# Two graph attention layers on one core: a prelude with another order of weight loads, strip copies and products

## The chip, the cores and the metric

The kernel runs on one core of a Trainium2 chip. The metric is the device time of one execution in microseconds (us); "before" and "after" are the same computation with and without the change. Lower is better. Single runs of this kernel differ by some per cent, so medians of several runs are compared.

## The reference

```python
def gnn0(x, adj):                       # Wf, Wg, W: 1024 x 1024
    f, g = x @ Wf + bf, x @ Wg + bg
    e = relu(f @ g.T)
    a = softmax(where(adj > 0, e, -9e15), axis=1)
    return a @ (x @ W + bW)

def gnn1(x, adj):                       # W1: 1024 x 1024, a1, a2: 1024 x 1
    h = x @ W1
    e = leaky_relu(h @ a1 + (h @ a2).T, 0.2)
    a = softmax(where(adj > 0, e, -9e15), axis=1)
    return relu(a @ h)

x = layernorm(x + gnn0(x, adj))
x = layernorm(x + gnn1(x, adj))
```

x is 2708 x 1024 in float32, adj is 2708 x 2708 in int32, mostly zero: a row has some 10 to 40 neighbours. Everything is float32.

## The kernel before, in words

The kernel does not multiply whole score matrices. It first makes, for every row, a list of its neighbours (at most CAP = 40), ranks the rows by the length of their lists into 85 groups of 32, and then gathers only the listed rows of x. The scores of layer 0 are x M x^T with M = Wf Wg^T, so that one product per row block, Fr, replaces f and g; the dots of Fr with the gathered rows are DVE's, the weighted sums of the gathered rows TensorE's.

All this change lies in the **prelude** (lists, ranks and M) and in the first steps of layer 0 behind it, together the first 250 us of the run. The prelude's work by engine:

- **adj blocks.** adj is cut into 21 full blocks of 128 rows (`full` = 21) and a short one of 20 rows. SP loads a full block (1354 KB) into one of BUFS = 4 buffers (`load_adj`, line 236). `keys` (550) has ACT turn it into float and sum each row, and POOL multiply it by a descending ramp, so that a neighbour becomes a key that tells its column. `maxima` (568) has DVE take the eight largest keys of each of 16 segments of a row (16 MAX8), and `best` (558) the 40 largest of these 128 (5 MAX8, 4 replacements) into L. `mixed` (577) weaves the MAX8 of one block with the `best` of the block before. The short block is laid out as 4 x 32 rows of 677 columns (`load_short` 595, `short_keys` 602, `short_maxima` 608), and its own `best` is woven in two blocks later. `keep_lists` (621) has ACT write a block's list in its final form and send it to memory.
- **M.** Wf and Wg come in 16 strips of 128 rows (512 KB) into KEPT = 5 slots (`load_weights`, 242), in the order Wg 0 to 3, Wf 0 to 5, Wg 4, Wf 6, Wg 5, Wf 7, Wg 6, Wg 7. `turned` (443) transposes a strip: 8 transposes on TensorE into two PSUM tiles called pt, which ACT copies into Wt (from Wf) or into a half of WgT (tiles halfT). `m_product` (466) makes 128 rows of M for one half of the columns in two times four matmuls; `c_product` (477) makes the bias rows, which ACT copies to cb and rb. The generator `weights` (510) is the order of all this: each `yield` tells a nominal length in us, and `work(upto)` (540) writes out steps until their nominal sum `spent` reaches `upto`. The copies that a step needs from ACT are kept in `late` and written out when the next step is. The bounds given to `work` thus set how the steps of M stand among the blocks' work, on each engine.
- **Ranks.** When all lists are made, `ranks` (326) works on DVE with three small products on TensorE; it stops at marks ("sums", "first", "hot", "second", "third", "end"), and `rank_to` (649) runs it to a mark. "first" is the place behind the first small product, "second" behind 22 small matmuls. It ends with ids and idq, the row numbers that the gathers use.
- **u rows.** `checks` (423) and `u_dots` (197) follow on DVE: each row strip of W1 is multiplied by a1 and a2. W1's strips 0 to 4 are loaded into the five strip slots, 5 and 6 into an adj buffer (lines 684 to 696), 7 into Wt when M is done (712).

Each engine runs its instructions in the order in which the program writes them (the class InOrder, line 61, adds that order as a dependency; nearly every instruction is therefore recorded on line 71). An instruction that waits holds everything behind it on its engine. SP's DMAs go round eight lanes, each of which waits for its last transfer.

The main loop (662) takes block b: ACT's and POOL's `keys(b + 2)`, lists of block b − 3, DVE's `mixed(b)`, the load of block b + 4 into the buffer that this frees, and then `work(6.2 * b - 6.0)`. Behind the loop come the ranks, with `work(124.0)` after the sums (697) and `work(135.0)` after the hot lists (703), and the rest of M in `work(1000.0)` (711).

Layer 0 starts with `load_x(1)` (1163), the gather of 128 rows of x by ids on POOL. Its tile xb lies at an address that an adj buffer had in the prelude. `half_product` makes the two column halves of x M for the first block, `take_half` (1184) copies a half into Fr, four copies for each of its four strips of 32 rows. DVE's first dots need Fr.

Of the kernel before, what the change touches and what calls it, by code (L numbers as in the profile page):

```python
# [8 lines left out]
F32 = mybir.dt.float32  # L9
# [97 lines left out]
def listed_path(ctx, tc, x, adj, Wf, bf, Wg, bg, W, bW, W1, a1, a2, out):  # L107

    nc = tc.nc
    P = 128  # L110
    N, D = x.shape
    KC = D // P
# [20 lines left out]
    pe, dve, act, pool, sp = (InOrder(tc, e) for e in (nc.tensor, nc.vector, nc.scalar, nc.gpsimd, nc.sync))  # L133
# [56 lines left out]
    M = wm.tile([P, KC, D], F32, name="M")  # L190
# [4 lines left out]
    Wt = s0s.enter_context(tc.tile_pool(name="w0", bufs=1, side="right")).tile([P, KC, D], F32, name="Wt")  # L195
# [23 lines left out]
    KEPT, BUFS = 5, 4  # L219
    with ExitStack() as prelude:  # L220
# [3 lines left out]
        stage, adjp = new_pool("stage", KEPT), new_pool("adjp", BUFS)  # L224
# [17 lines left out]
        def load_weights(upto):  # L242
            while len(loaded) < min(upto, len(order)):
                w, k = order[len(loaded)]
                t = stage.tile([P, D], F32, name="rows")
                sp.dma_start(t, w[k * P:(k + 1) * P, :])
                loaded.append(t)
# [190 lines left out]

        at = iter(range(len(order)))

        late, holders, WgT = [], [], {}

        def turned(dst):

            if any(take in holders for take in late):
                for take in late:
                    take()
                late.clear()
            n = next(at)
            t, pts = loaded[n], []  # L450
            for k0 in range(0, KC, 4):
                pt = ps_t.tile([P, 4, P], F32, name="pt")
                for i in range(4):
                    pe.transpose(pt[:, i, :], t[:, (k0 + i) * P:(k0 + i + 1) * P], ident)
                pts.append(pt)
            load_weights(n + 1 + KEPT)

            def take():
                for k0, pt in zip(range(0, KC, 4), pts):
                    act.copy(dst[:, k0:k0 + 4, :], pt)  # L460
            late.append(take)
            holders.append(take)
# [3 lines left out]
        def m_product(k, h):  # L466

            pm = ps_m.tile([P, H, 512], F32, name="pm")
            for i in range(KC):
                if i == KC // 2:  # L470
                    yield 3.5
                pe.matmul(pm[:, 0, :], Wt[:, i, k * P:(k + 1) * P], WgT[h][:, i, :],
                          start=(i == 0), stop=(i == KC - 1))
            late.append(lambda: act.copy(M[:, k, h * 512:(h + 1) * 512], pm[:, 0, :]))
            yield 3.5

        def c_product():

            pm = ps_m.tile([P, H, 512], F32, name="pm")
            for i in range(KC):  # L480
                if i == KC // 2:
                    yield 3.5
                for v, h in ((0, 0), (0, 1), (1, 0), (1, 1)):
                    j = 32 * (2 * v + h)
                    pe.matmul(pm[j:j + 32, 0, :], (bfc, bgc)[v][:, i:i + 1].to_broadcast([P, 32]),
                              Wt[:, i, h * 512:(h + 1) * 512] if v else WgT[h][:, i, :],
                              start=(i == 0), stop=(i == KC - 1))

            def take():
                for h in range(H):  # L490
                    act.copy(cb[32 * h:32 * h + 1], pm[32 * h:32 * h + 1, 0, :])
                for q in range(Q):
                    for h in range(H):
                        act.copy(rb[32 * q:32 * q + 32, h * 512:(h + 1) * 512], pm[64 + 32 * h:96 + 32 * h, 0, :])
            late.append(take)
            yield 3.5
# [13 lines left out]
        def weights():  # L510

            WgT[0] = wt0.tile([P, KC, 512], F32, name="halfT0")
            for k in range(4):
                turned(WgT[0][:, :, k * P:(k + 1) * P])
                yield 1.2
            WgT[1] = wt1.tile([P, KC, 512], F32, name="halfT1")
            turned(Wt[:, :, :P])
            yield 1.2
            for k in range(KC):
                if k + 1 < KC:  # L520
                    turned(Wt[:, :, (k + 1) * P:(k + 2) * P])
                    yield 1.2
                product = m_product(k, 0)
                yield next(product)
                if k >= 4:
                    turned(WgT[1][:, :, (k - 4) * P:(k - 3) * P])
                    yield 1.2
                yield next(product)
                if k == 0:
                    pt = ps_t.tile([P, 4, P], F32, name="pt")  # L530
                    pe.transpose(pt[:, 0, :16], two, ident[:16, :16])
                    late.append(lambda: act.copy(cols.rearrange("p v k -> p (v k)"), pt[:, 0, :16]))
                    holders.append(late[-1])
            yield from c_product()
            for k in range(KC):
                yield from m_product(k, 1)

        work_steps, spent = weights(), [0.0]

        def work(upto):  # L540

            while spent[0] < upto:
                old = list(late)
                spent[0] += next(work_steps, 1000.0)
                for take in old:
                    if take in late:
                        late.remove(take)
                        take()
# [46 lines left out]
        def load_short():  # L595

            for q in range(Q):
                sp.dma_start(short.bitcast(I32)[32 * q:32 * q + 32, :], adj[N - 32:N, q * PART:(q + 1) * PART])
            for h in range(H):
                sp.dma_start(cb[64 + 32 * h:65 + 32 * h], bW.rearrange("(o d) -> o d", o=1)[:, h * 512:(h + 1) * 512])  # L600
# [57 lines left out]
        keys(1)  # L658
        fill_highs()
        work(6.0)  # L660
        load_short()
        for b in range(full - 1):
            if b + 2 < full:
                keys(b + 2)
            if b == 3:
                short_keys()
            if b > 2:
                keep_lists(b - 3)
            if b == 9:
                keep_lists(NB - 1)  # L670
            others = [rest]
            if b == 4:
                short_maxima()
            if b == 6:
                others += [best(NB - 1, last, cand_s), short_total()]
            rest = mixed(b, *others)
            if b == 9:
                for t, a in ((u1b, a1), (u2b, a2)):
                    sp.dma_start(t, bass.AP(tensor=a.tensor, offset=a.offset, ap=[[0, P], [1, D]]))
            if b + BUFS < full:  # L680
                at_once(load_adj(b + BUFS))
            work(6.2 * b - 6.0)
            if b == full - 4:
                w1_rows = [stage.tile([P, D], F32, name="rows") for k in range(KEPT)]
                for k, t in enumerate(w1_rows):
                    sp.dma_start(t, W1[k * P:(k + 1) * P, :])

        t = adjp.tile([P, N], F32, name="adj")
        for k in range(KEPT, KC - 1):
            w1_rows.append(t[:, (k - KEPT) * D:(k - KEPT + 1) * D])  # L690
# [3 lines left out]
        keep_lists(full - 3)  # L694
        b = full - 1
        rank_to("sums")
        work(124.0)
        rank_to("first")
        at_once(rest)
        keep_lists(b - 1)  # L700
        final = maxima(b)
        rank_to("hot")
        work(135.0)
        rank_to("second", iter([next(final) for i in range(6)]))
        rank_to("third")
        rank_to("end", final)
# [43 lines left out]
    def half_product(pm, h, n, xT, w, row=None):  # L750
        c = slice(h * 512, (h + 1) * 512)
        for k in range(KC):
            pe.matmul(pm[:n, h, :], xT[:, k, :n], w[:, k, c],
                      start=(row is None and k == 0), stop=(k == KC - 1))
# [313 lines left out]
    with s0s:  # L1068
# [104 lines left out]
        halves = [ps_m.tile([P, H, 512], F32, name="pm") for h in range(H)]  # L1173
        xT1 = xTs.pop(1)
# [9 lines left out]
        def take_half(copy, ks, h):  # L1184
            c = slice(h * 512, (h + 1) * 512)
            for k in ks:
                for p in range(Q):
                    copy(Fr[1, k][32 * p:32 * p + 32, c], halves[h][32 * k:32 * k + 32, h, :])

        take_half(act.copy, (0, 1), 0)  # L1190
        take_half(act.copy, (2, 3), 0)
        xTs[2] = tp.tile([P, KC, P], F32, name="xT")
        turn2 = turn(xb[2], nrows[2], xTs[2])
        next(turn2)
        half_product(halves[1], 1, P, xT1, M, 0)
        q_dot(1)
        parts = xp.tile([P, D], F32, name="xb")
        small_f = split_product(xTs.pop(0), M, parts, 0, ps_s.tile([P, H, 512], F32, name="po"))
# [1 line left out]
        take_half(act.copy, (0, 1), 1)  # L1200
        for _ in turn2:
            pass
        next(small_f)
        take_half(act.copy, (2, 3), 1)
        f_product(2)
# [36 lines left out]
        for k, u in enumerate(units):  # L1242
            nxt = units[k + 1] if k + 1 < len(units) else None
            b = u.b
# [71 lines left out]
        b = NB - 1  # L1316
# [10 lines left out]
    with ExitStack() as s1s:  # L1327
# [106 lines left out]
        for n, (u, ks) in enumerate(parts):  # L1434
            b, po = u.b, banks[:, n % 2, :]
# [20 lines left out]
            if ks[-1] + 1 == u.G:  # L1456
                k = done1[b]
# [387 lines left out]
```

## Time and profile before

| what | us |
|---|---|
| median of three runs | 1885.37 |
| the three runs | 1868.06, 1885.37, 1900.10 |
| the profiled execution's own time | 1889.49 |
| its span, first to last instruction | 1887.8 |
| block 4's MAX8 start on DVE | 52.38 |
| TensorE: bias rows (c_product) | 115.82 to 122.8 |
| ranks start on DVE | 149.37 |
| gather of the first rows of x on POOL | 194.63 |
| first dots on DVE | 223.09 |

The profile is of one execution, and its own time is 1.7 us over its span. An engine's row in the timeline gives start, length, engine, line, operation, output and input, and in brackets how long the engine stood idle before it and what released it. In the waits, `A <- B: 25.2, 4, 19.1` means that A waited for B four times, 25.2 us in all and 19.1 at most. In the names, xb are the gathered rows of x, pt and pm PSUM tiles, adj a block of adj, cand the 128 candidates of a row, u2b the tile in which the short block lies until a2 is loaded there.

### The profile page before, as it was taken

The numbers are of one execution on the slowest core, as the hardware profiler recorded it, in microseconds if no ns is written. First come the engines' busy times: TensorE is split into PE (matmuls) and PEld (weight loads), VectorE is DVE, ScalarE is ACT, GpSimd is POOL, SyncE is SP. The second block draws the span as 40 slices with busy tenths as digits, with TensorE's granted clock in tenths as the row PEclk, the third lists the DMA queues.
The fourth block names the chain that finished last, engine by engine and source line by source line (L and its number), as shares of the span: only waits on it lengthen the run. The fifth ranks groups of instructions, "written<-read, shape, count | busy, mean of one in ns | idle before, by whom it ended". The sixth has DMA issues, their size and how long they took to land. (4 is left out here: it accounts for less than half of the span.)

```text
span 1887.8 us, 22782 instructions
## 1 busy us (share of the span) xinstructions
PE 1614.6 (86%) x6873; PEld 684.2 (36%) x6873; DVE 1279.9 (68%) x4158; ACT 637.6 (34%) x886; POOL 1180.3 (63%) x1130
## 2 busy tenths in 40 slices
PE   3898759788999999999999998279898988989896
PEld 2443324333443444444444443023333333323332
DVE  5996648767888888888888767246445445545543
ACT  5571425434554544444555551011111111111111
POOL 8892673555676777766767631666666666666630
PEclk7999889888999999999999999589999999989998
DMA  9671583656787778887777863999989999999950
GB/s 365 227 284 50 193 293 116 223 176 238 284 278 270 277 251 274 280 281 262 262 257 263 310 239 136 342 329 320 321 319 348 351 347 317 343 333 352 341 190 35
DMA packets 150961, 503.95 MB, mean 267 GB/s; under 512 B 32714, under 2 KB 32730, under 8 KB 148398
## 3 DMA queue, kind: packets, MB, share of 16 engines
q0 software_dynamic: 131648, 428.27, 63.9%
q1 hardware_dynamic: 16128, 73.71, 10.5%
q8 instruction: 56, 0.92, 0.2%
q10 hardware_dynamic: 3054, 0.43, 0.1%
q14 instruction: 75, 0.61, 0.1%
HBM read 510.81 MB, written 33.75 MB: 288 GB/s over the span
## 5 line engine op out<-in xcount | busy, mean ns | idle before, releaser
L71 POOL DMA_INDIRECT ring<-in_x_dram,SL x405 | 447.2, 1104 | 210.7 <-issue 95.1
L71 DVE SCALAR_TENSOR_TENSOR j<-ring,Fr 128x1024 bf16<-128x1024 f32 x402 | 493.1, 1227 | 100.3 <-ACT Fr L71 41.9
L71 PE MATMUL po<-ring,st 128*32 128x512 f32 x2616 | 376.9, 629 | 109.9 <-issue 56.2
L71 ACT COPY Fr<-pm 32x1024 f32<-32x1024 f32 (+2 forms) x353 | 340.6, 965 | 15.1 <-remote 6.5
L71 POOL DMA_INDIRECT ring<-T,SL x249 | 246.9, 992 | 122.9 <-issue 64.5
L71 PE MATMUL pm<-M,yT 128*128 128x512 f32 (+1 forms) x704 | 318.2, 601 | 4.5 <-issue 3.0
L71 PE MATMUL pm<-Wt,xT 128*128 128x512 f32 (+1 forms) x704 | 305.8, 603 | 12.2 <-issue 12.2
L71 PE MATMUL pm<-M,xT 128*128 128x512 f32 x672 | 298.5, 603 | 2.4 <-issue 2.4
L71 PEld LDWEIGHTS po<-ring,st 128*32 128x32 f32 x2616 | 109.4, 115 | 322.3 <-issue 258.6
L71 POOL DMA_INDIRECT more<-T,SL x156 | 155.0, 993 | 76.9 <-issue 42.8
L71 PEld LDWEIGHTS pm<-M,yT 128*128 128x128 f32 (+1 forms) x704 | 127.7, 187 | 195.7 <-issue 192.9
L71 PEld LDWEIGHTS pm<-Wt,xT 128*128 128x128 f32 (+1 forms) x704 | 131.2, 189 | 175.0 <-issue 171.1
L71 ACT ACTIVATE scores<-scores 128x12 f32<-128x12 f32 (+9 forms) x65 | 14.0, 216 | 520.2 <-DVE scores L71 415.2
L71 PEld LDWEIGHTS pm<-M,xT 128*128 128x128 f32 x672 | 130.5, 194 | 160.9 <-issue 158.2
L71 POOL TENSOR_TENSOR adj<-adj,iota 128x2708 f32<-128x2708 f32 (+2 forms) x23 | 124.5, 5446 | 17.0 <-ACT adj L71 17.0
L71 ACT ACTIVATE y<-po,ri 128x512 f32<-128x512 f32 (+1 forms) x88 | 58.1, 684 | 211.7 <-remote 134.4
L71 PE MATMUL pm<-halfT,Wt 128*128 128x512 f32 x256 | 114.3, 602 | 0.0
L71 POOL DMA_INDIRECT SL<-LD,idq x85 | 88.4, 1040 | 28.4 <-issue 25.8
L71 PE MATMUL po<-more,st 128*32 128x512 f32 x624 | 94.0, 659 | 13.2 <-issue 13.1
L71 DVE MAX8 cand<-adj 128x8 f32<-128x170 f32 x336 | 95.9, 325 | 12.4 <-POOL adj L71 12.4
L71 ACT COPY xT<-pt 128x512 f32<-128x512 f32 (+2 forms) x109 | 47.9, 499 | 85.6 <-PE pt L71 56.7
L71 POOL DMA_INDIRECT z<-in_x_dram,ids x21 | 25.1, 1194 | 81.3 <-DVE j L71 26.3
(236 smaller groups left out, 1436.0 us busy)
## 6 DMA issues: line engine op xcount, KB each, us to landing
adj<-in_adj_dram SPq DMA_DIRECT2D x19, 1354.0 KB
X1S<-z SPq DMA_DIRECT2D x19, 512.0 KB
ring<-in_x_dram,SL POOLq DMA_INDIRECT x405
rows<-in_L_gnn_Wg_dram SPq DMA_DIRECT2D x8, 512.0 KB
rows<-in_L_gnn_Wf_dram SPq DMA_DIRECT2D x8, 512.0 KB
M<-in_L_gnn_W_dram SPq DMA_DIRECT2D x1, 4096.0 KB
ring<-T,SL POOLq DMA_INDIRECT x249
u1b<-X1S SPq DMA_DIRECT2D x7, 512.0 KB
```

The costliest lines, as they stand in the source:

```text
L71: made = self.tc.keep_in_program_order(op(*args, **kwargs))
```

## The change

The strips of weights are no longer asked for by the transposing of an earlier strip but one or two a block, right behind the load of an adj block, and never more than five ahead of those transposed. The copies of Wf's strip 0 are written out before the loop. The short block is loaded at block 1, its MAX8 stand at block 6 and its `best` at block 8, each two later, as are the last block's `keep_lists` and the loads of a1 and a2. Wf's strip 1 is transposed behind the first half of M's first product. The bounds of `work` in the loop are 16 us higher, up to 118.0; `work(124.0)` is gone, and 135.0 becomes 128.0. One more adj tile is named before the one that takes W1's strips. In layer 0 the second column half of the product is written before the transposes of the third block's rows, and the copies of Fr's strip 3 after them.

```diff
--- before.py
+++ after.py
@@ -438,7 +438,7 @@
 
         at = iter(range(len(order)))
 
-        late, holders, WgT = [], [], {}
+        late, holders, WgT, turned_so_far = [], [], {}, [0]
 
         def turned(dst):
 
@@ -447,13 +447,14 @@
                     take()
                 late.clear()
             n = next(at)
+            load_weights(n + 1)
             t, pts = loaded[n], []
             for k0 in range(0, KC, 4):
                 pt = ps_t.tile([P, 4, P], F32, name="pt")
                 for i in range(4):
                     pe.transpose(pt[:, i, :], t[:, (k0 + i) * P:(k0 + i + 1) * P], ident)
                 pts.append(pt)
-            load_weights(n + 1 + KEPT)
+            turned_so_far[0] = n + 1
 
             def take():
                 for k0, pt in zip(range(0, KC, 4), pts):
@@ -517,11 +518,14 @@
             turned(Wt[:, :, :P])
             yield 1.2
             for k in range(KC):
-                if k + 1 < KC:
+                if 0 < k and k + 1 < KC:
                     turned(Wt[:, :, (k + 1) * P:(k + 2) * P])
                     yield 1.2
                 product = m_product(k, 0)
                 yield next(product)
+                if k == 0:
+                    turned(Wt[:, :, P:2 * P])
+                    yield 1.2
                 if k >= 4:
                     turned(WgT[1][:, :, (k - 4) * P:(k - 3) * P])
                     yield 1.2
@@ -658,7 +662,9 @@
         keys(1)
         fill_highs()
         work(6.0)
-        load_short()
+        for take in late:
+            take()
+        late.clear()
         for b in range(full - 1):
             if b + 2 < full:
                 keys(b + 2)
@@ -666,25 +672,29 @@
                 short_keys()
             if b > 2:
                 keep_lists(b - 3)
-            if b == 9:
+            if b == 11:
                 keep_lists(NB - 1)
             others = [rest]
-            if b == 4:
+            if b == 6:
                 short_maxima()
-            if b == 6:
+            if b == 8:
                 others += [best(NB - 1, last, cand_s), short_total()]
             rest = mixed(b, *others)
-            if b == 9:
+            if b == 11:
                 for t, a in ((u1b, a1), (u2b, a2)):
                     sp.dma_start(t, bass.AP(tensor=a.tensor, offset=a.offset, ap=[[0, P], [1, D]]))
             if b + BUFS < full:
                 at_once(load_adj(b + BUFS))
-            work(6.2 * b - 6.0)
+            if b == 1:
+                load_short()
+            load_weights(min(KEPT + b + 1 + max(0, b - 3), turned_so_far[0] + KEPT))
+            work(min(6.2 * b + 10.0, 118.0))
             if b == full - 4:
                 w1_rows = [stage.tile([P, D], F32, name="rows") for k in range(KEPT)]
                 for k, t in enumerate(w1_rows):
                     sp.dma_start(t, W1[k * P:(k + 1) * P, :])
 
+        adjp.tile([P, N], F32, name="adj")
         t = adjp.tile([P, N], F32, name="adj")
         for k in range(KEPT, KC - 1):
             w1_rows.append(t[:, (k - KEPT) * D:(k - KEPT + 1) * D])
@@ -694,13 +704,12 @@
         keep_lists(full - 3)
         b = full - 1
         rank_to("sums")
-        work(124.0)
         rank_to("first")
         at_once(rest)
         keep_lists(b - 1)
         final = maxima(b)
         rank_to("hot")
-        work(135.0)
+        work(128.0)
         rank_to("second", iter([next(final) for i in range(6)]))
         rank_to("third")
         rank_to("end", final)
@@ -1188,11 +1197,11 @@
                     copy(Fr[1, k][32 * p:32 * p + 32, c], halves[h][32 * k:32 * k + 32, h, :])
 
         take_half(act.copy, (0, 1), 0)
-        take_half(act.copy, (2, 3), 0)
+        take_half(act.copy, (2,), 0)
+        half_product(halves[1], 1, P, xT1, M, 0)
         xTs[2] = tp.tile([P, KC, P], F32, name="xT")
         turn2 = turn(xb[2], nrows[2], xTs[2])
         next(turn2)
-        half_product(halves[1], 1, P, xT1, M, 0)
         q_dot(1)
         parts = xp.tile([P, D], F32, name="xb")
         small_f = split_product(xTs.pop(0), M, parts, 0, ps_s.tile([P, H, 512], F32, name="po"))
@@ -1200,6 +1209,7 @@
         take_half(act.copy, (0, 1), 1)
         for _ in turn2:
             pass
+        take_half(act.copy, (3,), 0)
         next(small_f)
         take_half(act.copy, (2, 3), 1)
         f_product(2)
```

## The prediction

> **What bounds the kernel now.** The page comes first: its engine line and the chain that ended last.
>
> ```profile
> PE 1614.6 (86%) x6873; PEld 684.2 (36%) x6873; DVE 1279.9 (68%) x4158; ACT 637.6 (34%) x886; POOL 1180.3 (63%) x1130
> PE 33%; issue 5%; DVE 2%; DMA 1%; ACT 1%; POOL 1%; another core or an unknown queue 0%; POOLq 0%; DVEq 0%; ACTq 0%
> ```
>
> TensorE sets the long stretch: it is busy 86% and leads the chain. The change touches only the first 262 us of 1887.8. There TensorE is busy 9.6 of the first 40 us and 30.3 of the 50 us from 150 to 200 (the windows view), so other waits set the pace. I ask the waits of that stretch next (what waits, for whom: us in total, times, longest).
>
> ```profile
> POOL xb L71 <- DVE iota L71: 40.6, 1, 40.6
> PE pt L71 <- ACT Wt L71: 25.2, 4, 19.1
> POOL adj L71 <- ACT adj L71: 17.0, 9, 4.3
> DVE j L71 <- ACT Fr L71: 14.5, 1, 14.5
> DVE halfT L71 <- PE pt L71: 14.1, 2, 8.0
> DVE u2b L71 <- POOL u2b L71: 11.0, 1, 11.0
> ```
>
> Read backwards, they name the path: the first dots on DVE wait for Fr (14.5), Fr for the gather of x, the gather for DVE (40.6), and DVE, while ranking, twice for TensorE (14.1). Before that DVE waits for POOL's short block (11.0). TensorE waits 19.1 for one copy by ACT. The timeline by engine shows why (start, length, what, idle before it and its releaser).
>
> ```profile
> 38.44 1.97 PE L71 MATMUL pt<-ident,rows 128*128 128x128 f32 x8 [19.13 <-ACT Wt L71]
> 57.02 1.04 PE L71 MATMUL pt<-ident,rows 128*128 128x128 f32 x8
> 164.18 13.98 PE L71 MATMUL pm<-halfT,Wt 128*128 128x512 f32 x32
> ```
>
> ```profile
> 35.36 2.46 ACT L71 ACTIVATE adj<-adj 128x2708 f32<-128x2708 int32 x1 [9.27 <-DVE cand L71]
> 37.82 1.05 ACT L71 COPY Wt<-pt 128x512 f32<-128x512 f32 x2
> ```
>
> ```profile
> 28.70 6.22 SPq L71 DMA_DIRECT2D adj<-in_adj_dram  x3
> ```
>
> The copy of Wf's strip 0 (37.82) stands behind ACT's work on block 4 of adj (35.36). That block's load goes out only at 28.70, behind five strips of Wf and the short block's loads on SP's queue. TensorE loses 19 us and then trails with M to the end of the ranking, where two of its products stand in front of the ranks' own small ones:
>
> ```profile
> 51.41 1.05 DVE L71 MAX8 u2b<-u2b 128x8 f32<-128x170 f32 x4 [10.97 <-POOL u2b L71]
> 164.40 0.39 DVE L71 TENSOR_TENSOR halfT<-halfT,pt 128x220 f32<-128x220 f32 x1 [6.09 <-PE pt L71]
> 179.32 0.24 DVE L71 COPY halfT<-pt 64x85 f32<-64x85 f32 x1 [8.02 <-PE pt L71]
> ```
>
> ```profile
> 101.86 29.65 POOL L71 TENSOR_TENSOR adj<-adj,iota 128x2708 f32<-128x2708 f32 x5 [2.63 <-ACT adj L71]
> 194.63 2.08 POOL L71 DMA_INDIRECT xb<-in_x_dram,ids  x1 [40.57 <-DVE iota L71]
> ```
>
> A block costs POOL 29.65/5 = 5.93 us and DVE about as much: from 52.38 DVE has work without a break to the ranks at 149.37, 97.0 us with the short block's own list.
>
> **The sum** is made on the profiled execution: 1889.5 us, span 1887.8 and 1.7 around it, 4.1 above the median of three, 1885.4.
>
> **Loads, Wf0's copies, second strip.** The same strips and blocks are loaded, in another order. Block 4 needs only the buffer of block 0, whose last MAX8 ends at 14.5. An adj block keeps the DMA engines busy some 3.3 us when loads follow one another (successive blocks' landings 20.27 and 23.53), a strip 512/1354 of that, 1.3. So block 3 lands at 23.5, block 4 at 26.9, Wf1 at 28.2, block 5 at 31.6, the four short loads at 32.9, Wf2 at about 34.4. On TensorE five strips are through by 20, the first half of M's step 0 runs 20.4 to 24.0, Wf1 28.2 to 30.1, the second half to 34.0, Wf2 34.4 to 36.2 (1.94 a strip after a wait). ACT has Wf2's two copies before block 4: 36.9. Block 4 then runs on ACT to 39.5 and on POOL to 45.4. That is 39.5 for POOL's start against 37.99: **1.5 later**, the price of the strip in front of it.
>
> **The short block's lists two blocks later.** DVE no longer waits for POOL's product of the short block before block 4. It starts block 4 at 45.4, not 52.38: **−7.0**. Its four MAX8 (1.05) are done at block 6, when their data lies long ready: +1.0 before the ranks. The longer list (best of the short block) and the loads of a1 and a2 move within DVE's unbroken stretch and SP's queue: nothing; there they have until the first u_dots, 187.1 and more. The last block's keep_lists moves too, one ACTIVATE (0.37) and its DMA, in ACT's slack; if ACT had none, 0.4.
>
> **Strips behind adj's loads.** Each later strip is asked for when DVE releases a block, behind that block's load: 5.4 to 6.0 us from issue to ACT's use (58.82 to 64.80, 64.23 to 70.21), then 1.3. By that rule Wf5 lands at 58.3 and is needed at 59.0, Wf6 64.3 (67.6), Wf7 73.7 (76.3), the strips of Wg 3.7 to 9 us ahead. Nothing, but Wf5's cover is 0.7 us; if it is gone every later product is late by as much. TensorE runs from 36.2 through seven products (6.86 each, 48.0), nine strips (0.87 when no wait, 7.8) and the row sums (7.0), to about 99: 23 earlier than 122.8.
>
> **ACT's cluster.** After the row sums ACT copies cb and rb, 1.16 + 4.71 = 5.9 us in one piece. They now come at 100, behind block 14, and block 15's keys end at about 109. POOL, at 5.93 a block from 39.5 and 1.6 for the short one, wants them at 106.1: 2.9 late. DVE runs about 2 behind POOL once it has done the short list, so I take **+1.3** for DVE, between 0 (enough lag) and 2.9 (none). Ranks start at 45.4 + 1.0 + 97.0 + 1.3 = **144.7**, not 149.37.
>
> **M's end in the ranks.** The bounds of TensorE's work change to 118 in the loop, none at "sums" and 128 before "second". Built in this order, 44 matmuls of half 1 stand before the ranks' first product, 12 between it and the second, 8 after. One takes 41.47/48 = 0.86. The 44 are 38 us: over at 138, ten before the sums (144.7 + 3.85 = 148.5), so the first wait (6.09) goes; late next is DVE itself. The 12 are 10.3, from 148.5 to 158.8, and 1.7 for a cold start (16 rows of product took 8.72 after the long wait, 7.03 warm): 160.6. DVE, with neither wait, arrives at 144.7 + 8.94 + 6.9 = 160.5. With the 22 small matmuls (1.19) the copy starts at 161.8, not 179.32: **−17.5**, which holds all terms so far. The other 8 matmuls (6.9, cold 8.6) follow the constant's product at about 166.5 and end at 175; TensorE's next need is x's transposes, 200.25 − 17.5 = 182.8. That cover is 8 us; without it they would cost 6.9. W1's last strip, loaded after them, is needed only after the first dots.
>
> **The new adj tile** before W1's rows. In both built programs the tile that holds W1's rows 5 and 6 covers the same addresses, and the first block's x still overlaps it: the gather still waits for four u_dots (1.27 each). I cost it at nothing; bounds: 0 and, if the gather were free, −6.5 (rival B).
>
> **Order of Fr's copies.** The second half of the product stands behind z's transposes, and one of four groups of copies (4 × 0.59) moves behind x's next transposes. Fr's first strip is whole 2.4 us earlier at most. ACT feeds the dots' 14.5 us wait directly (copies 211.26 to 225.38), so I take **−2.0**, between 0 and −2.4. The fourth group now stands between the second half's; the dots that want it are later than those of strips 0 and 1.
>
> Sum: −17.5 − 2.0 = −19.5; 1889.5 − 19.5 = 1870.0, and 4.1 lower beside the median: **1866**. After the prelude every step follows from the gather of x, so the gain should stay.
>
> Beside the strip's 0.87 and 1.04 us stands a rule that speaks against them. The Trainium skill, "TensorE: Matmul & The Clock Gate", section "Part 4: PE-mode transpose", says that transposes don't count as TensorE work for the fast clock and that the full clock does not engage in them. The trace shows 1.04 right behind products and 1.94 to 1.97 behind waits, so here it disagrees; by the rule the sum would be 1874, as in rival F.
>
> **Rivals.**
> A, the forecast: 1866.
> B, the gather of x is really clear of W1's rows. Then x comes after the ids (165) and M's last copy (175) ends last instead of 182.8: at most 7.8, I take 6.5 more: 1859. For it: the wait of 40.6 is named after DVE's u_dots. Against it: the addresses.
> C, ACT's order paces the blocks. Copies of strips stand ahead of blocks on ACT, so POOL's waits (17.0 in nine pieces) don't shrink but grow. If the ranks start at 152 (7 late, half a us for each block), the rank waits still go: 152 + 3.85 + 12 + 1.2 = 169 against 179.3, −10.3, and Fr −1.5: 1889.5 − 11.8 − 4.1 = 1874.
> D, the other side: a closed loop. DVE frees a buffer, SP loads a block and a strip (5.9 + 1.3), TensorE turns it behind one or two products (2.0 + 6.9 or 13.7), ACT copies (1.1) and only then does the next block's keys (2.65), POOL 5.93: 25.5 or 32.3, against 4 × 5.93 = 23.7 for four buffers. With two products on the way in each turn it is 8.1 a block, 2.15 more; over 13 blocks +28, less the 18 that the rest still brings: 1885.4 + 10 = 1895. It decides from 1.5 us a block. Against it: strips come ahead of need by the working above, so the copies don't wait a whole turn.
> E, the gain is not handed on: the long stretch, led by TensorE, has 28% gaps for other waits that a different start may open: 1885.
> F, strips always at 1.94: nine times 1.07 is 9.6 more before cb and rb, which then meet block 16 or 17, and POOL's wait grows from 2.9 to about 9: some 7.5 of the 19.5 are lost, −12: 1874.
>
> **How the numbers follow.** A 0.55, C 0.20, E 0.08, B 0.07, D 0.06, F 0.04. The likeliest gives 1866. Single runs of before lie from 1868.1 to 1900.1, some 16 us to either side, so a median of a few can miss a true 1866 by about ten. 1848 to 1887 takes in A, B, C, E and F with most of that spread; D and the outer tails are left out, below 2 in 10. Two per cent, about what a measurement of this kernel can tell from no change, is 37.7 us: 1847.7 and 1923.1. Below the first only A's and B's tails lie, 0.11; above the second part of D and a stray median, 0.06; within 0.83.
>
> **What would show it.** Right: TensorE's 19.1 us wait for Wt gone, its transposes of Wf1 near 28; DVE's 10.97 gone and block 4 at about 45; row sums over near 100; POOL waiting for ACT once after cb and rb, about 3; ranks from 144.7 and no wait over 2 us in them for TensorE; x's gather at about 177, still released by DVE; the dots' wait for Fr near 12.5. Wrong: strips that TensorE waits for (C, D), ranks from 149 or later, the gather before the u_dots (B), transposes of 1.9 right behind products (F), or all this and the same total (E).

## The result, and the profile after

| | before | after |
|---|---|---|
| median of 22 runs of each, us | 1889.7 | 1873.3 |
| ratio, with its 95% interval | | 0.9923 [0.9902, 0.9945] |
| span of the profiled execution | 1887.8 | 1869.0 |
| block 4's MAX8 start on DVE | 52.57 | 44.99 |
| bias rows done on TensorE | 122.9 | 100.0 |
| ranks start on DVE | 149.37 | 143.92 |
| copy behind the second mark | 179.32 | 160.88 |
| first gather of x | 194.63 | 176.20 |
| first dots on DVE | 223.09 | 201.86 |
| DVE takes the next rows of x | 262.15 | 242.53 |

The kernel is 0.8% faster, 14.6 us of 1889.7 (10.4 to 18.5 by the interval); the forecast was 19.5 less than before, which from the median of three runs then known (1885.4) gave 1866. The 52.38 of the table before is a MAX8 of block 3's `best`, which stands in front of block 4's first at 52.57. Ratios leave disturbed executions out; the traces of two experiments below, e1_take_back and e7_rank_bounds_only, come from disturbed ones, so only their first 250 us are read.

The waits of the same stretch of the changed kernel, 0 to 262 us (us in total, times, longest):

```profile
POOL xb L71 <- DVE iota L71: 27.7, 1, 27.7
...
POOL adj L71 <- ACT adj L71: 11.7, 4, 4.4
DVE j L71 <- ACT Fr L71: 11.5, 1, 11.5
...
DVE j L71 <- DMA xb<-in_x_dram,ids: 11.1, 1, 11.1
...
PE pt L71 <- DMA rows<-in_L_gnn_Wf_dram: 4.7, 1, 4.7
...
DVE halfT L71 <- PE pt L71: 1.3, 1, 1.3
```

Gone are TensorE's wait for ACT's copy (25.2 in four) and DVE's for the short block (11.0). The ranks' waits for TensorE shrank from 14.1 to 1.3. New is TensorE's wait of 4.7 for Wf's strip 1. The 11.1 that DVE waits for xb is the wait for the second gather of x, behind the first dots (9.5 before). TensorE's timeline, changed kernel:

```profile
28.05 1.94 PE L71 MATMUL pt<-ident,rows 128*128 128x128 f32 x8 [4.67 <-DMA rows<-in_L_gnn_Wf_dram]
...
147.33 0.17 PE L71 MATMUL pt<-halfT,lower 128*128 128x10 bf16 x1 [9.34 <-DVE halfT L71]
...
147.80 11.93 PE L71 MATMUL pm<-halfT,Wt 128*128 128x512 f32 x24
```

TensorE now waits 9.3 us for the ranks; before, the ranks waited for it. (The trace has two records for each of M's matmuls, so x24 are 12 of them.) ACT's, DVE's and POOL's timelines, changed kernel:

```profile
35.40 1.07 ACT L71 COPY Wt<-pt 128x512 f32<-128x512 f32 x2 [0.65 <-PE pt L71]
36.36 2.47 ACT L71 ACTIVATE adj<-adj 128x2708 f32<-128x2708 int32 x1
```

```profile
44.99 0.34 DVE L71 MAX8 cand<-adj 128x8 f32<-128x170 f32 x1 [4.29 <-POOL adj L71]
...
56.51 1.04 DVE L71 MAX8 u2b<-u2b 128x8 f32<-128x170 f32 x4
...
114.65 0.34 DVE L71 MAX8 cand<-adj 128x8 f32<-128x170 f32 x1 [0.90 <-POOL adj L71]
...
160.88 0.24 DVE L71 COPY halfT<-pt 64x85 f32<-64x85 f32 x1 [1.33 <-PE pt L71]
```

```profile
52.37 53.22 POOL L71 TENSOR_TENSOR adj<-adj,iota 128x2708 f32<-128x2708 f32 x9
108.67 35.38 POOL L71 TENSOR_TENSOR adj<-adj,iota 128x2708 f32<-128x2708 f32 x6 [3.09 <-ACT adj L71]
...
176.20 2.09 POOL L71 DMA_INDIRECT xb<-in_x_dram,ids  x1 [27.70 <-DVE iota L71]
```

The short block's MAX8 (56.51) have no wait. POOL runs nine blocks without a break and then waits 3.09 behind ACT's cb and rb; DVE waits 0.90 for the block that this delays (114.65). The gather of x is still released by DVE's product on W1's rows (iota is that product's scrap output).

### The profile page after: what moved, and what is told of

Same layout as the page of the kernel before. It is cut to its first block, busy times and chain, and to the rows that moved or that the text cites. A ratio compares the mean times of both kernels' runs of the same rounds, so it can differ in the third digit from the quotient of the medians.

```text
span 1869.0 us, 22758 instructions
## 1 busy us (share of the span) xinstructions
PE 1609.9 (86%) x6851; PEld 684.0 (37%) x6873; DVE 1277.7 (68%) x4158; ACT 636.5 (34%) x886; POOL 1174.6 (63%) x1130
## 3 DMA queue, kind: packets, MB, share of 16 engines
q1 hardware_dynamic: 16128, 73.71, 10.6%
## 5 line engine op out<-in xcount | busy, mean ns | idle before, releaser
L71 POOL DMA_INDIRECT ring<-in_x_dram,SL x405 | 442.4, 1092 | 213.8 <-issue 94.4
L71 PE MATMUL po<-ring,st 128*32 128x512 f32 x2616 | 366.3, 616 | 103.8 <-issue 42.8
L71 ACT COPY Fr<-pm 32x1024 f32<-32x1024 f32 (+2 forms) x353 | 340.6, 965 | 24.4 <-remote 15.9
L71 PE MATMUL pm<-M,yT 128*128 128x512 f32 (+1 forms) x704 | 324.9, 605 | 16.2 <-issue 14.1
L71 PE MATMUL pm<-Wt,xT 128*128 128x512 f32 (+1 forms) x704 | 299.9, 593 | 3.5 <-issue 2.9
L71 ACT ACTIVATE scores<-scores 128x12 f32<-128x12 f32 (+9 forms) x65 | 14.1, 216 | 549.0 <-DVE scores L71 446.7
L71 PEld LDWEIGHTS pm<-M,xT 128*128 128x128 f32 x672 | 130.4, 194 | 160.9 <-issue 157.9
L71 POOL TENSOR_TENSOR adj<-adj,iota 128x2708 f32<-128x2708 f32 (+2 forms) x23 | 124.3, 5440 | 11.7 <-ACT adj L71 11.7
L71 ACT COPY yT<-pt 128x256 f32<-128x256 f32 (+1 forms) x86 | 27.6, 373 | 136.4 <-PE pt L71 109.7
```

Source lines behind the costliest of these rows:

```text
L71: made = self.tc.keep_in_program_order(op(*args, **kwargs))
```

## The experiments

Three calls of four kernels; those of a call ran on one chip and share its runs of the kernel before. "Gather" is the first gather of x, "dots" the first dots on DVE, in the kernel's trace. Beside them stand the trace of before (194.63, 223.09) and two of the changed kernel (176.20, 201.86; in the third call 178.86, 205.36).

| kernel | ranks | second mark | gather | dots | ratio to before |
|---|---|---|---|---|---|
| e1_take_back | 144.11 | 162.46 | 177.78 | 206.53 | 0.9940 [0.9881, 0.9998] |
| e4_short_only | 141.80 | 171.18 | 186.50 | 216.20 | 0.9990 [0.9937, 1.0043] |
| e5_copies_only | 149.34 | 179.59 | 194.91 | 223.58 | 1.0052 [0.9999, 1.0105] |
| e7_rank_bounds_only | 149.04 | 172.42 | 187.75 | 216.68 | 0.9986 [0.9929, 1.0042] |
| e2_short_back | 154.51 | 171.54 | 186.86 | 212.68 | 0.9978 [0.9944, 1.0013] |
| e9_loads_back | 144.68 | 164.12 | 179.45 | 206.12 | 0.9852 [0.9751, 0.9953] |
| e8_u_first | 144.57 | 163.19 | 173.13 | 196.73 | 0.9891 [0.9850, 0.9932] |
| e10_short_rank | 141.97 | 164.62 | 179.94 | 208.80 | 0.9905 [0.9869, 0.9941] |
| after_again | 144.92 | 163.53 | 178.86 | 205.36 | 0.9902 [0.9885, 0.9919] |
| e11_rank_fill | 144.71 | 160.27 | 175.57 | 202.21 | 0.9900 [0.9886, 0.9914] |
| e12_fill_u_first | 144.18 | 159.74 | 169.66 | 194.75 | 0.9892 [0.9873, 0.9911] |
| e13_delay | 144.28 | 162.75 | 198.34 | 224.91 | 1.0012 [1.0001, 1.0023] |

In the first call the intervals reach some 10 us to either side, so the ratios there can't tell whether a gain of 7 or 8 us at the gather comes out at the end; for single parts only the marks in the traces are read.

### One part alone on the kernel before

**e4_short_only**: the short block's lists two blocks later.

```diff
-            if b == 9:
+            if b == 11:
                 keep_lists(NB - 1)
...
-            if b == 4:
+            if b == 6:
                 short_maxima()
-            if b == 6:
+            if b == 8:
                 others += [best(NB - 1, last, cand_s), short_total()]
...
-            if b == 9:
+            if b == 11:
                 for t, a in ((u1b, a1), (u2b, a2)):
```

> The kernel before with the short block's lists two blocks later and nothing else. Theory that two paths must both be shortened: block 4 starts on DVE at about 45 and the ranks at 143 instead of 149.4, but TensorE is as late as before, so the waits for it grow from 14 to about 20 us and x's gather stays between 191 and 195; total 1886 to 1890. Rival, that DVE's blocks alone set the end: gather at 188.5 and total 1883.

The gather came 8.1 earlier, past both expectations, and the theory is wrong in one half: the ranks start 7.6 earlier, but TensorE's bias rows come 9.5 earlier too (113.4 instead of 122.9), with its order of work untouched. DVE frees the adj buffers sooner, so SP loads and ACT's keys come sooner, and with them the strip copies that stand between the keys. The ranks' waits stay nearly as they were (6.09 and 8.02 before):

```profile
156.26 0.38 DVE L71 TENSOR_TENSOR halfT<-halfT,pt 128x220 f32<-128x220 f32 x1 [5.64 <-PE pt L71]
...
171.18 0.24 DVE L71 COPY halfT<-pt 64x85 f32<-64x85 f32 x1 [8.02 <-PE pt L71]
```

**e5_copies_only**: the copies of Wf's strip 0 before the loop.

```diff
         work(6.0)
+        for take in late:
+            take()
+        late.clear()
         load_short()
```

> The kernel before with the copies of Wf's strip 0 written out before the loop and nothing else. TensorE's wait of 19.1 goes, M's first product comes about 9 earlier, but the next copies still stand behind ACT's block keys. Theory: most of the 9 is lost again by the bias rows (before 115.8 to 122.8), they come 2 to 5 earlier, and x's gather 2 to 5 (190 to 193). Rival, that the one copy is the whole of TensorE's lateness: bias rows 9 or more earlier, gather at 186 or less.

Nothing is left of it; the 2 to 5 us expected were too much as well. TensorE's timeline and its waits for ACT's copies:

```profile
25.07 1.94 PE L71 MATMUL pt<-ident,rows 128*128 128x128 f32 x8 [5.39 <-DMA rows<-in_L_gnn_Wf_dram]
26.81 8.94 PE L71 MATMUL pm<-halfT,Wt 128*128 128x512 f32 x16
```

```profile
PE pt L71 <- ACT Wt L71: 14.9, 5, 8.4
```

The largest wait in TensorE's list was removed and its first product came 13.4 earlier (26.81 for 40.20), yet the bias rows end at 123.2 for 122.9. The next copies stand behind ACT's next keys, and these have not moved: TensorE's other waits for copies grew from 6.1 (25.2 less 19.1) to 14.9.

**e7_rank_bounds_only**: only the bounds behind the loop.

```diff
         rank_to("sums")
-        work(124.0)
         rank_to("first")
...
-        work(135.0)
+        work(128.0)
```

> The kernel before with only the bounds behind the loop changed: no steps of M at the sums, 128 instead of 135 before the second mark. Four steps of 4 matmuls (13.7 us) no longer stand before the ranks' first product, so the first wait (6.1) goes; then five steps (17.2) stand before the second. Theory: second mark at about 170.5 instead of 178.1, x's gather about 7.5 earlier, 187; total about 1880. Rival, that the ranks' order matters only with an earlier TensorE: gather within 2 of 194.6.

Nearly as the theory had it: second mark 172.42 (170.5 expected; 20 matmuls took 17.4), gather 6.9 earlier (7.5 expected).

**e10_short_rank**: the edits of e4_short_only and e7_rank_bounds_only together, and no other.

> The kernel before with the short block's lists two blocks later and the bounds behind the loop changed, nothing else: neither loads nor strip copies nor Fr's order. Measured alone, the two moved x's gather by 8.1 and 6.9. Theory: they add up, since TensorE's 36 matmuls end at 144 ahead of the sums at 145.7, and 20 follow: second mark at 164, gather at 179.5, first dots at 208, total 1871. Rival, that without the earlier copies TensorE stands in the way again: gather 184 or later.

They add up: second mark 164.62, gather 179.94, 14.7 earlier of the full change's 18.4, and the ratio is that of the full change within its interval. The other parts (loads in the loop, strips and copies moved, a higher bound in the loop) brought 1 to 4 us more at the gather (178.86 and 176.20). TensorE's long wait is still there:

```profile
PE pt L71 <- ACT Wt L71: 18.0, 1, 18.0
```

So four fifths of the gain at the gather came without removing it.

### One part taken from the changed kernel

**e2_short_back**: the edits of e4_short_only undone.

> The changed kernel with the short block's lists in the old places (MAX8 at block 4, its best at 6). Theory: block 4 on DVE waits for POOL's short keys again, starts at 53.4 instead of 45.0, one us of MAX8 is then already done, and the ranks start at about 151.3; TensorE is ahead, so x's gather moves as much: 183.5 instead of 176.2, total 1880. Rival, that TensorE's early M alone brings the gain: gather within 2 of 176.

Ranks at 154.51, 3 later than expected and even 5 later than before. POOL's and TensorE's timelines say why:

```profile
72.23 5.95 POOL L71 TENSOR_TENSOR adj<-adj,iota 128x2708 f32<-128x2708 f32 x1 [7.98 <-ACT adj L71]
```

```profile
67.14 1.94 PE L71 MATMUL pt<-ident,rows 128*128 128x128 f32 x8 [8.88 <-DMA rows<-in_L_gnn_Wf_dram]
```

```profile
53.61 6.22 SPq L71 DMA_DIRECT2D u2b<-u2b  x8
59.94 0.41 SPq L71 DMA_DIRECT2D adj<-in_adj_dram  x1
60.45 0.37 SPq L71 DMA_DIRECT2D rows<-in_L_gnn_Wf_dram  x1
```

Rival D's loop is here: DVE waits for the short block, so its eight small copies go out late, at 53.61 on SP's queue, and with them the adj load and Wf's strip behind them. In the kernel before they go out as late (52.49), but there the strips that TensorE turns next (57.02, 64.77) had been asked for long before, and it does not wait for them. Here TensorE waits 8.88 for that strip, ACT's copies wait for TensorE, and POOL's block waits 7.98 for ACT, whose queue has the copies in front. So with the short block in its old place the new rule of loading holds the ranks up. The new rule alone was not run; the time of this kernel (0.9978) can't be told from that of the one before.

**e9_loads_back**: the old rule of loading in the changed kernel.

```diff
             n = next(at)
-            load_weights(n + 1)
...
-            turned_so_far[0] = n + 1
+            load_weights(n + 1 + KEPT)
...
-            load_weights(min(KEPT + b + 1 + max(0, b - 3), turned_so_far[0] + KEPT))
```

> The changed kernel with the old rule of loading (each transposing asks for the strip five ahead, nothing asked for in the loop), everything else as changed. adj block 4 is then behind five strips again and lands at about 35 instead of 27, but Wf's strips are there early, so TensorE does not wait for them. Theory: ACT's block 4 starts at 35 to 37 as it does now (36.4), and all later marks stay within 1.5: gather 175 to 177.5, total 1873. Rival, that the order of loads carries the gain: block 4 late, gather 182 or more.

Ranks at 144.68 and gather at 179.45, between 0.6 and 3.2 later than the two traces of the changed kernel, which differ by 2.7 themselves; at most 177.5 was expected, 182 or more by the rival. Block 4 starts on DVE at 41.9, even 3.1 earlier, and that is lost again at ACT's copies of cb and rb: behind them DVE waits 3.85 (at 115.39), where it waits 0.90 in the changed kernel. The order of the loads carries little or nothing of the gain at the gather; the ratio's interval is too wide to add to that.

**e1_take_back**: Fr's copies and the second column half in the old order.

```diff
-        take_half(act.copy, (2,), 0)
-        half_product(halves[1], 1, P, xT1, M, 0)
+        take_half(act.copy, (2, 3), 0)
...
         next(turn2)
+        half_product(halves[1], 1, P, xT1, M, 0)
...
-        take_half(act.copy, (3,), 0)
```

> The changed kernel with Fr's copies and the second column half in the order of before (part 8 undone). If that order is worth what the two traces show (first dots 21.23 earlier, gather of x 18.43), x's gather stays at 176 and the first dots come 2.8 us later, 204.7 instead of 201.9; the total about 1876. If the 2.8 come from TensorE's clock or the gathers instead, the dots stay at 202 and the total at 1873.

From gather to dots it takes 28.75 (before: 28.46), against 25.66 in the changed kernel's first trace and 26.50 in its second: the new order is worth 2 to 3 us there. From the gather to DVE's use of the next rows of x it is 67.6 (before 67.5) against 66.3 and 65.2, so 1.3 to 2.4 would be left of it 40 us later. But e9_loads_back, which has the new order, takes 68.7 there, so this remainder is not shown. What it is worth at the end, the ratio's interval does not tell.

### Beyond the change

**e8_u_first**: the four products that the gather waits for, ahead of the last block's list.

```diff
         score_constant()
+        junk = iota.bitcast(BF16)[:, :D]
+        u_dots(2 * KEPT, U1, lambda k: w1_rows[k], junk)
         at_once(rest)
         keep_lists(b)
...
-        junk = iota.bitcast(BF16)[:, :D]
         checks()
-        u_dots(2 * KEPT, U1, lambda k: w1_rows[k], junk)
```

> The changed kernel with the four products on W1's strips 5 and 6, for whose tile the first gather of x waits, ahead of the last block's list and the checks (5.5 us of DVE's work). Theory: the gather comes 5.5 earlier, 170.7; x's transposes at 176.3, just behind M's last product (175.7); first dots at 196.4 instead of 201.9; total 1868. Rival, that the lists' gathers or M's last product take its place: dots no earlier than 200.

The gather stands 9.9 behind the second mark, not 15.3, and the dots come at 196.73 as expected. But DVE's timeline goes on with

```profile
245.03 1.23 DVE L71 SCALAR_TENSOR_TENSOR j<-xb,rb 128x1024 bf16<-128x1024 f32 x1 [14.77 <-DMA xb<-in_x_dram,ids]
```

where the changed kernel waits 11.08 until 242.53. The last list goes to memory later (ACT issues it at 176.33 instead of 169.12). The gathers of lists, which read it, gain less than the gather of x: the first comes at 180.54 instead of 182.16, though the gather of x is 3.1 earlier. POOL waits 3.58 before it, and the profile names no releaser, so the late list is the likely cause and not a shown one. POOL's next gather of x is 2.5 later (239.12 for 236.60). The dots were 5 us earlier, the next rows of x were not.

**after_again**, the changed kernel once more, and three variants beside it.

> The changed kernel as it is, beside the three that follow: x's gather at 176 to 178, first dots at 202 to 204, total some 15 below the kernel before.

Gather and dots came 0.9 and 1.4 later than the latest expected, the total 17.0 below the kernel before.

**e11_rank_fill**: TensorE's pause before the ranks filled.

```diff
         rank_to("sums")
+        work(127.0)
         rank_to("first")
...
-        work(128.0)
+        work(134.0)
```

> The changed kernel with 52 of M's matmuls before the ranks' first product (44 now), 8 before the second (12 now), 4 at the end. TensorE stands idle 9.3 us before the sums now and its 12 matmuls then take 11.9 to 13.6 instead of 10.3. Theory: the 8 more end at 145, still ahead of the sums (147.3); the pause shrinks to 2.4 and the 8 go at the warm rate, 6.9; the second mark is DVE's, at 159.6, and x's gather comes at 174.9, 1.3 earlier than in the first trace of the changed kernel and 2.5 to 3 earlier than in those with a slow start. Rival, that the 52 end after the sums: gather at 177 or later.

Gather 3.3 earlier than in after_again, though the 8 matmuls took 8.8 and not 6.9; the ratio is the same, with an interval of 0.0014 (2.4 us) to either side. In its trace all of POOL's gathers are earlier than in after_again's, by 3 to 7 us up to 800 us of the run and by 1.5 to 2.7 behind 950.

**e12_fill_u_first**: both edits.

> Both: 52, 8 and 4 matmuls, and the four products on W1's strips 5 and 6 ahead of the last list. Theory: gather at 169.5 (174.9 less 5.4), M done at about 169, x's transposes at 175, first dots at 193.3; total 5 to 8 below the changed kernel of the same call. Rival, that the gathers of the lists then set the dots: dots at 196 or later.

Gather 9.2 and dots 10.6 earlier than in after_again; the total, expected 5 to 8 lower, the same (0.9892 and 0.9902, 1.7 us apart, each known to 3). Of the 10.6, 3.9 are left where DVE takes the next rows of x (240.10 for 244.04), as in e8_u_first. POOL's gathers of lists and rows are 2.6 to 6.3 earlier until 330 us, and by 433 us 0.3; on the way DVE waits 6.2 us in ten pieces for gathered rows, 1.8 in two in after_again. No version of these beats the changed kernel by more than its interval.

**e13_delay**: 16 more products in front of the gather.

```diff
         checks()
-        u_dots(2 * KEPT, U1, lambda k: w1_rows[k], junk)
+        for i in range(5):
+            u_dots(2 * KEPT, U1, lambda k: w1_rows[k], junk)
```

> The changed kernel with 16 more products on W1's strips 5 and 6 on DVE (the same four, four times again) in front of the first gather of x: a delay of 16 x 1.27 = 20.3 us at the gather and nothing else. It measures what of a shift of the start comes out at the end. Theory of the prediction: all, total 20 above the changed kernel of the same call. Rival, that later stages absorb a part: 10 to 16.

The gather moved by 19.5 from after_again and the time by 19.1 (ratios 1.0012 and 0.9902 of 1734.7) or 20.9 (medians 1737.2 and 1716.3): all of it. So a delay of all gathers on POOL by 20 us comes out in full. That an advance of some us does is not shown by these variants: e11_rank_fill and e12_fill_u_first had the gathers earlier and no lower time that their intervals can tell.

## Why the prediction was right, point by point

- **Path and mechanism.** Right at the ranks and the gather, but TensorE's long wait, which the prediction puts at the start of the path, is not what held the end: e10_short_rank keeps 18.0 of it, e5_copies_only removes it for nothing. What counts is how much of M stands in front of the ranks' products and when DVE is through with the blocks. The ranks and the gather moved as forecast: ranks 143.92 (144.7), second mark 160.88 (161.8), gather −18.4 (−17.5). The gather is still released by DVE's products, so rival B is out; strips never ran at 1.9 right behind products (1.04 a strip), so F is out. E, no gain at all, is out by the interval. Its 28% of gaps is not what the windows give: TensorE is busy 1124.7 of the 1280 us from 600 to 1880, 88%. Of C and D, C's growing waits did not come (POOL's 17.0 in nine became 11.7 in four), and D's loop shows in e2_short_back, where the short block's move is missing (its terms as listed add to 25.8 and 32.6, not 25.5 and 32.3; nothing hangs on that).
- **Loads.** Wf's strip 1 came at 28.05 as worked out, and block 4 on DVE at 44.99 (45.4). e9_loads_back shows that the old rule would have done as well: the prediction did not say so.
- **The short block, −7.0 +1.0.** Right at its place. It is worth more than the prediction's step said: by itself 8.1 at the gather, since TensorE follows DVE through the adj buffers and ACT's queue (e4_short_only).
- **ACT's cluster, +1.3.** POOL waited 3.09 as worked out (2.9), and DVE 0.90 for the block behind it (114.65); in after_again it is 1.5. Right for this kernel, inside the range of 0 to 2.9. The cost hangs on where the blocks stand when the cluster comes: 0.19 in e10_short_rank, 3.9 in e9_loads_back. DVE's only other wait from block 5 to the ranks was 0.62, at 58.36.
- **M's end in the ranks.** The first wait went, the second shrank to 1.33, TensorE waits 9.34. The cold start was put at 1.7; the 12 matmuls took 11.93 to 13.60 in seven traces with the same 44 and 12, against 10.3: 1.6 to 3.3. The 161.8 lies inside what was measured (160.9 to 164.1 where the ranks start at 144 to 145), but that the first trace came within 0.9 of it is in part luck: it has the shortest of these cold starts.
- **Fr's order, −2.0.** The dots gained 2.8 (21.23 − 18.43), outside the 0 to 2.4 given: 16 copies stand before the first dots, not 20, and the first half of the product ran 0.4 faster. But summing this step to the end was not justified: e12_fill_u_first had the dots 10.6 earlier and no lower time that its interval can tell.
- **"The gain should stay."** For the gather's part most of it did, and a delay there comes out in full (e13_delay). Against the 18.4 that the gather gained, the two sets of timed runs give 14.6 (10.4 to 18.5) and, in the third call, 17.0 (14.1 to 19.9; 0.0098 of 1734.7).

The forecast time missed by 7.3 us. Of that 4.3 is the base: the median of before is 1889.7 in 22 runs, not the 1885.4 of three. The rest fits the dots' part (2.0) and the width of the interval, but is not told apart. Single traces have a noise of that size too: between 300 and 430 us the shift of POOL's gathers goes from −20.6 to −8.0 and back to −18 in the first pair of traces, around a copy for which ACT waits 15.9 us (before 6.5) on something that the profile does not name. What that is stays open.

## What to carry to other kernels

The longest wait of an engine need not be worth anything: 19 us of TensorE's were removed alone and nothing came of it, because its next input stood behind work of another engine that had not moved. In a ring of engines that share a few buffers, look for the one whose late release holds the others (here DVE waiting for a small side block), and move that first: with the two bounds behind the loop it gave four fifths of what the whole change gave at the gather. And an earlier first use of a result counts for little if the transfers behind it are not earlier too.

## What the runs showed of the hardware

**The clock after a pause.** Windows of the changed kernel around the sums, and of e11_rank_fill (after the busy times: granted TensorE clock, DMA share, GB/s):

```profile
140.00:145.00 5.00, 0.00 (x0) 0.00 (x0) 4.83 (x23) 0.36 (x1) 4.92 (x3) 0.54 0.18 55
...
148.20:150.00 1.80, 1.80 (x3) 0.75 (x3) 1.63 (x8) 0.00 (x0) 0.30 (x1) 0.50 0.04 6
150.00:152.00 2.00, 2.00 (x5) 0.78 (x4) 1.90 (x6) 0.37 (x1) 0.00 (x0) 0.85 0.02 2
152.00:154.00 2.00, 2.00 (x7) 0.81 (x6) 1.83 (x8) 0.00 (x0) 0.00 (x0) 1.00 0.07 11
```

```profile
145.00:148.20 3.20, 0.69 (x3) 0.17 (x2) 3.12 (x6) 0.00 (x0) 2.98 (x4) 1.00 0.01 1
148.20:150.00 1.80, 1.52 (x4) 0.86 (x4) 1.66 (x8) 0.00 (x0) 1.04 (x2) 0.60 0.03 2
150.00:152.00 2.00, 2.00 (x3) 0.67 (x2) 1.86 (x8) 0.37 (x1) 0.00 (x0) 0.50 0.03 6
152.00:154.00 2.00, 2.00 (x6) 0.95 (x5) 1.90 (x5) 0.00 (x0) 0.00 (x0) 1.00 0.10 16
```

In the long pause the clock is halved, 2.4 us after TensorE's last matmul there, and it is full again 2.8 us after M's work has begun. In e11_rank_fill TensorE stood still only some 3 us (145.6 to 148.6, with two tiny products in between), and the clock was halved all the same, just as the work began again. So filling the pause to within 3 us bought no warm start. How long the cold state lasts varies: in nine traces of the changed kernel and its variants the clock fell 2.0 to 5.2 us after the last matmul of the 44 or 52 and was full again 2.8 to 6.2 us after M's next matmul. Half the clock over 2.8 us costs 1.4, over 6.2 us 3.1: so the same 12 take 11.93 us in one trace and 13.60 in another, against 10.3. The Trainium skill, "TensorE: Matmul & The Clock Gate", section "What's actually happening", puts the cold state behind at least one idle window of about 3.4 us and the warm one behind about as much sustained work. The traces agree in the order of size only: most of the falls came sooner, after 2.0 to 3.0 us, and most of the rises later.

**The calls differ.** In the third call, on another chip, the kernel before took 1734.7 (17 runs, 1729.1 to 1738.8), 8% less than in the first two. Up to the first dots the traces of the changed kernel differ by 3.5 us; the difference builds up later, more than half of it behind layer 0, where the two traces show (last column GB/s), first here and then in the third call:

```profile
1250.00:1600.00 350.00, 307.15 (x1349) 121.21 (x1348) 176.90 (x881) 49.26 (x105) 233.32 (x304) 0.97 0.92 329
```

```profile
1100.00:1500.00 400.00, 355.98 (x1694) 141.78 (x1698) 239.11 (x1139) 58.70 (x134) 308.34 (x393) 0.94 1.00 381
```

The gathers there move 381 GB/s at a DMA share of 1.00, against 329 at 0.92. Times are therefore compared within a call alone. Whether it is the chip or its state at the hour was not tried.
